# A recurrent-attention and lookup-table FFN block on one core: first gates turned by TensorE, statistics two slots ahead, sums of LN(x)^T at their own products, lookup steps dealt out anew

## The chip, the cores and the metric

The kernel runs on one core of a Trainium2 chip, in one launch. The metric is device time in microseconds (us). The kernel before was run three times: 2121.52, 2121.64 and 2123.93 us, median 2121.64.

## The reference, cut to what matters

```
x: (8, 1024, 512) fp32
xn  = (x - mean) / sqrt(var + 1e-5)                        # LN over the 512
# attention: D = 128, three decays
q, k_i, v_i = xn @ Wq, xn @ Wk[i], xn @ Wv[i];  gate = softmax(xn @ Wg)
w_i[t, s] = sigmoid(decay_logits[i]) ** max(s - t - 1, 0) * (s > t)
s   = sum_i gate[..., i] * ((q @ k_i^T) * w_i) @ v_i;  s = s @ Wo * out_scale
# FFN whose weights are table look-ups: w = lut[idx], lut of 16, idx (1376, 512) and (512, 1376)
g   = silu(down(silu(gate(xn)) * up(xn)))
out = x + s * g
```

Everything is fp32.

## The kernel before, in words

The kernel has two phases. Phase 1 (some 600 us) normalises and transposes x, makes the projections, runs the attention recurrence and builds the FFN weights from the table into DRAM. Phase 2 (the other 1500 us) is the FFN with the weights streamed back, and the output. Matrix products are by Strassen's scheme in Winograd's form: seven products of halves, with sums of the operands made beforehand. The diff touches phase 1 alone.

Phase 1 walks through batches b = 0 to 8 and, in each, through eight *slots* k = 0 to 7, one chunk of 128 tokens each, last chunk first (c = 7 - k). In a slot generators are advanced by hand, each by a step at a time:

- `newer`, `project(b)`, three steps per slot. Step 1: `transpose(c)` (four transposes `pt` on TensorE, ScalarE copies them to `xnT`), `normalize(c - 1)`, `statistics(c - 2)`, loads of x. Step 2, from slot 4 on: a product of `features(1)`. Step 3: `values(c)` (`pv`, copied to `v_sb` by ScalarE) and a further product of `features(1)`. In slot 4 also the softmax of the gates of tokens 512 to 1023.
- `ending`, the second half of `project(b - 1)`: in slots 0 to 3 the same for `features(0)`, whose products run while the next batch is transposed.
- `older`, `chunks(b - 1)`, three steps per slot: transposes `pk` of the keys, scaled by ScalarE into `ks` (L630); then `psc` (scores), VectorE's `pr` (L636), and for the next chunk `ga` (L611) by VectorE and `qb` (L615) by GpSimd; then the state product `pu` (needs `ks`) and the output `po` (needs `pr`), copied by ScalarE (L659, L663, L670).
- `weights`, the table look-ups: 396 steps in all. A look-up of one block is three bit masks (L218), one index step (L221), eight leaves (L225) and seven selects (L242), all on VectorE, most of them over 128 x 1024; after it come steps in which only GpSimd works (the Strassen sums, L272 to L301). `build_some(n)` takes n of these steps; it stands in three places of a slot.
- `following`, the start of `project(b + 1)`: first loads and statistics of the next batch.

`features(hf)` is one Strassen product of q and the three k for 512 tokens. Its products run in the order 1, 5, 6, 2, 7, 3, 4, one per step, thus two per slot over four slots; they accumulate in PSUM banks `pa`, `pe`, `pb`, `pa`, `pc`, `pe`, `pc`. Their right-hand operands are quarters of LN(x)^T or the sums `t1` (L494, for product 5), `t2` (L498, for 6), `t3` (L503, for 7) and `t4` (L509, for 4) that VectorE makes; VectorE also adds `c22` (L516, after product 7) and `c12` (L519, after product 3). `there` is a store of these for phase 2.

`statistics` of batches from 1 on are two passes of ScalarE (L411, L412) and two small steps of GpSimd that give `rstd` (L413, L414); `normalize` is two ScalarE steps (L421, L422).

The gates, softmaxed as 128 tokens x 12, are needed as 12 rows broadcast to all partitions: stored to DRAM element by element (L458), then read back by a broadcast (L462). `defer(n, ...)` issues something n `tick()`s later; a slot has three ticks.

The order on TensorE, VectorE, ScalarE and GpSimd is the order in which the program is traced (`keep_order` ties each instruction to the one before). SyncE's queue is tied so up to slot (0, 3) alone; after that the framework's planner places its DMAs.

Of the kernel before, what the change touches and what calls it, by code (L numbers as in the profile page):

```python
# [9 lines left out]
F32 = mybir.dt.float32  # L10
# [7 lines left out]
P = 128  # L18
# [30 lines left out]
def recurrent_block(ctx: ExitStack, tc, x, wq, wk, wv, wo, wg, decay_logits, out_scale, lut, gidx, uidx, didx, out):  # L49
# [84 lines left out]
    def defer(parts, issue):  # L134
        later.append([parts, issue])
# [241 lines left out]
    def project(b, pools, sides, kept):  # L377
# [61 lines left out]
        def softmax(hf):  # L439

            n = NC // NHALF
            logits = gt[:, ts(hf, n), :]
            g = small.tile([P, n, NI], F32, name=f"g{b}_{hf}", tag="g")
            red = small.tile([P, n, 1], F32, name=f"red{b}_{hf}", tag="red")
            nc.vector.tensor_reduce(red, logits, AX.X, ALU.max)
            nc.vector.tensor_tensor(g, logits, red.to_broadcast([P, n, NI]), ALU.subtract)
            nc.scalar.activation(g, g, AF.Exp)
            yield
            sm = small.tile([P, n, 1], F32, name=f"sm{b}_{hf}", tag="sm")
            nc.vector.tensor_reduce(sm, g, AX.X, ALU.add)  # L450
            nc.vector.reciprocal(sm, sm)
            nc.vector.tensor_tensor(g, g, sm.to_broadcast([P, n, NI]), ALU.mult)
            gates.append(att.tile([P, n * NI, P], F32, name=f"ga{b}_{hf}", tag="ga"))
            there = gT_d[b][ts(hf, n * NI), :]

            def write():
                with nc.allow_non_contiguous_dma(reason="1536 words"):
                    nc.sync.dma_start(out=there.rearrange("k p -> p k"), in_=g.rearrange("p c i -> p (c i)"))  # L458

            ga = gates[-1]  # L460
            defer(2, write)
            defer(6, lambda: nc.sync.dma_start(out=ga, in_=there.partition_broadcast(P)))  # L462

        def features(hf):

            qk[hf] = att.tile([P, NI + 1, U], F32, name=f"qk{b}_{hf}", tag=f"qk{hf}", bufs=1)  # L470
            c11, c12, c21, c22 = (qk[hf][:, 2 * j : 2 * j + 2, ts(c, H)] for j in (0, 1) for c in (0, 1))
            ts_ = tp.tile([P, 4, 2, H], F32, name=f"ts{b}_{hf}", tag=f"ts{hf}")
            b11, b12, b21, b22 = (xnT[:, 2 * v : 2 * v + 2, ts(2 * hf + c, H)] for v in (0, 1) for c in (0, 1))
            t1, t2, t3, t4 = (ts_[:, k] for k in range(4))
            a11, a12, s3, a22 = (wqk_sb[:, 2 * v : 2 * v + 2, ts(j, 2 * D)] for j in (0, 1) for v in (0, 1))
            s1, s2, s4 = (wqs[:, k] for k in range(3))
            lhs = {1: a11, 2: a12, 3: s4, 4: a22, 5: s1, 6: s2, 7: s3}
            rhs = {1: b11, 2: b21, 3: b22, 4: t4, 5: t1, 6: t2, 7: t3}
            pa, pb, pe, pc = (p_a.tile([P, 2, H], F32, name=f"{r}{b}_{hf}", tag=r) for r in ("pa", "pb", "pe", "pc"))

            def product(ps, k, start=False):
                for j in range(2):
                    for v in range(2):
                        nc.tensor.matmul(  # L484
                            ps[:, j, :],
                            lhsT=lhs[k][:, v, ts(j, D)],
                            rhs=rhs[k][:, v, :],
                            start=start and j == 0 and v == 0,
                            stop=False,
                            skip_group_check=True,  # L490
                        )

            there = xs_d[b][:, :, ts(hf, H)]
            nc.vector.tensor_tensor(t1, b12, b11, ALU.subtract)  # L494
            yield
            product(pa, 1, True)
            nc.scalar.copy(pb, pa)
            nc.vector.tensor_tensor(t2, b22, t1, ALU.subtract)  # L498
            nc.sync.dma_start(out=there[:, 0:4, :], in_=xnT[:, :, ts(2 * hf, H)])
            yield  # L500
            product(pe, 5, True)
            nc.scalar.copy(c21, pe)
            nc.vector.tensor_tensor(t3, b22, b12, ALU.subtract)  # L503
            nc.sync.dma_start(out=there[:, 4:6, :], in_=b22)
            yield
            product(pb, 6)
            nc.scalar.copy(pc, pb)
            nc.scalar.copy(c12, pb)
            nc.vector.tensor_tensor(t4, b21, t2, ALU.subtract)  # L509
            defer(2, lambda: nc.sync.dma_start(out=there[:, 6:14, :], in_=ts_.rearrange("p a b u -> p (a b) u")))  # L510
            yield
            product(pa, 2)
            nc.scalar.copy(c11, pa)
            yield
            product(pc, 7)
            nc.vector.tensor_tensor(c22, pc, c21, ALU.add)  # L516
            yield
            product(pe, 3)
            nc.vector.tensor_tensor(c12, pe, c12, ALU.add)  # L519
            yield  # L520
            product(pc, 4)
            nc.scalar.copy(c21, pc)
            yield
# [3 lines left out]
        def load_to(c):  # L527
            nonlocal ahead
            while ahead >= max(c, 0):
                load(ahead)  # L530
                ahead -= 1

        if b == 0:
            load_to(NC - 1)
            yield
            load_to(NC - 4)
        else:
            load_to(NC - 4)
        statistics(NC - 1)
        if b > 0:  # L540
            yield
            load_to(NC - 5)
        normalize(NC - 1)
        statistics(NC - 2)
        yield
        lag = 1 if b == 0 else 0
        for k in range(NC):
            c = NC - 1 - k
            transpose(c)
            if c > 0:  # L550
                normalize(c - 1)
            if c > 1:
                statistics(c - 2)
            if (b, k) != (0, 0):
                load_to(c - 5)
            if b == 0 and k == 0:
                warm_up(5)
            yield
            if k == NC // 2:
                if lag:  # L560
                    values(c + 1)
                    lag = 0
                of_half = features(1)
                next(of_half)
            if k >= NC // 2:
                next(of_half)
            half = softmax(1) if k == NC // 2 else iter(())
            next(half, None)
            yield
            next(half, None)  # L570
            if k >= lag:
                values(c + lag)
            if k >= NC // 2:
                next(of_half, None)
            yield
# [99 lines left out]
    def phase_1():  # L675
        nonlocal small, p_a, p_c, p_r
        with (
# [22 lines left out]
            def build_some(n):  # L700
                for _ in range(n):
                    next(weights, None)
# [12 lines left out]
            for b in range(B + 1):  # L715
                following = project(b + 1, pools, sides, kept) if b + 1 < B else iter(())
                older = chunks(b - 1, (chk, blp), kept) if b else iter(())
                for k in range(NC):

                    short = b > 0 and k % 4 == 3  # L720
                    busy = (b > 0 or k >= NC // 2) and b < B
                    swap = (b, k) == (1, 0)
                    tick()
                    next(newer, None)
                    next(older, None)
                    next(setup, None)
                    build_some((b, k) > (0, 0) and 1 + (0 < b < B) - short)
                    next(more, None)
                    tick()
                    if k < NC // 2:  # L730
                        for _ in range(2):
                            next(ending, None)
                    next(newer, None)
                    build_some(busy * (1 + (b > 0) - short))

                    next(newer if swap else older, None)
                    build_some(busy * (2 + (b > 0) + (b > 0 and k % 4 == 0)))
                    if k < NC // 2:
                        next(ending, None)
                    if k >= NC - 2:  # L740
                        next(following, None)
                    tick()
                    next(older if swap else newer, None)
                    next(older, None)
                    if (b, k) == (0, 3):
                        sums_of_weights(wqk_sb, wqs)
                        keep_order(tc, seen, (mybir.EngineType.SP,))
                for g in (older, ending):
                    for _ in g:
                        pass  # L750
                ending, newer = newer, following
# [669 lines left out]
```

## Time and profile before

| what | value |
|---|---|
| median of three runs | 2121.64 us |
| the profiled execution | 2122.92 us |
| its span, first to last instruction | 2121.0 us |
| instructions in the span | 32177 |
| mean granted TensorE clock | 0.996 |
| spacing of slots without a wait, from transpose to transpose | 9.50 us; 7.78 from slot 3 to 4; 6.78 after slot 7 |
| slot (1, 0) | 44.40 to 61.34, 16.95 us |

The times in the profile count from the span's start. PE is TensorE's matmul, PEld its weight load, DVE VectorE, ACT ScalarE, POOL GpSimd, SP SyncE. L434 is line 434 of the kernel. A line `A <- B: 12.8, 6, 5.1` in a list of waits says that A's engine stood idle 12.8 us before A, in 6 places, at most 5.1 us at once, until B was done. Lines of a timeline have start, duration, engine, line, operation and tiles, and in brackets the idle time before.

### The profile page before, as it was taken

The page shows a single profiled execution, that of the slowest core. Times are in us where ns is not written, and L with a number is a line of the kernel's source. Part 1 is how long each engine was busy: PE and PEld are TensorE (multiplying, and loading weights), DVE is VectorE, ACT ScalarE, POOL GpSimd, SP SyncE. Part 2 cuts the span into 40 slices and gives each one's busy share as a digit, 9 for nine tenths or more (in the row PEclk, how much of TensorE's full clock was granted, in tenths as well). Part 3 has the DMA queues.
Part 4 walks back from the last instruction along what each step waited for, and adds up shares of the span by engine and source line. Part 5 has one row for each costly group of instructions (what it writes and reads, how often), then busy time and mean ns, then how long its engine had stood idle before and what let it go on. Part 6 is the DMA issues. An engine that isn't in the chain of part 4 may idle for free.

```text
span 2121.0 us, 32177 instructions
## 1 busy us (share of the span) xinstructions
PE 2090.8 (99%) x11690; PEld 1756.3 (83%) x11690; DVE 1440.2 (68%) x2214; ACT 943.8 (44%) x2115; POOL 1038.9 (49%) x1050
## 2 busy tenths in 40 slices
PE   9999999999999999999999999999999999999999
PEld 6778777888878888888879888887978888797877
DVE  7789887799735775566567556655755675675557
ACT  4657765776534424423441442244145324423531
POOL 3555555364544537516542752655275256527432
PEclk9999999999999999999999999999999999999999
DMA  8575686647764654463455446344644634464443
GB/s 189 159 167 189 144 202 188 152 151 158 158 198 152 231 185 152 157 241 129 155 190 191 144 152 246 131 153 166 215 146 158 242 124 158 165 217 147 153 153 109
DMA packets 186163, 361.51 MB, mean 170 GB/s; under 512 B 52467, under 2 KB 123766, under 8 KB 186006
## 3 DMA queue, kind: packets, MB, share of 16 engines
q1 hardware_dynamic: 171446, 335.20, 51.1%
q0 software_dynamic: 4480, 14.68, 1.7%
q10 hardware_dynamic: 10080, 9.58, 1.5%
q8 instruction: 93, 1.52, 0.3%
q14 instruction: 64, 0.52, 0.1%
HBM read 282.87 MB, written 76.55 MB: 169 GB/s over the span
## 4 chain that ended last, share of the span: by engine, by line
PE 88%; DVE 5%; DMA 2%; POOL 2%; ACT 1%; issue 1%; SPq 0%; DVEq 0%; POOLq 0%; ACTq 0%
PE s L865 33%; PE sE L865 6%; PE pv L434 5%; PE s12d L1119 5%; PE s21d L1119 5%; PE s11d L1119 5%; PE fs L813 3%; PE pd L1232 3%; PE ps L1239 3%; PE po L658 2%; PE sEd L1119 2%; PE pc L484 2%; PE pe L484 2%; PE pa L484 2%; PE fsE L813 1%; DMA x<-in_x 1%
## 5 line engine op out<-in xcount | busy, mean ns | idle before, releaser
L865 PE MATMUL s<-xs,wq 128*128 128x256 f32 x3264 | 731.2, 379 | 0.0
L865 PEld LDWEIGHTS s<-xs,wq 128*128 128x128 f32 x3264 | 619.5, 190 | 95.9 <-issue 8.4
L888 DVE TENSOR_TENSOR s<-s,e 128x512 f32<-128x512 f32 x136 | 95.1, 699 | 204.3 <-ACT s L887 204.2
L1203 POOL TENSOR_TENSOR cu<-cu 128x256 f32<-128x256 f32 x32 | 34.8, 1087 | 306.7 <-DVE cl L1202 304.5
L434 PE MATMUL pv<-wvg_sb,xnT 128*128 128x387 f32 x512 | 177.4, 488 | 0.0
L796 POOL TENSOR_TENSOR xs<-xs 128x256 f32<-128x256 f32 x224 | 170.9, 790 | 7.1 <-PE fs L813 2.5
L892 DVE TENSOR_TENSOR sE<-s,e 128x512 f32<-128x512 f32 x136 | 95.0, 699 | 104.6 <-PE s L865 104.6
L956 POOL TENSOR_TENSOR u<-u,e 128x512 f32<-128x512 f32 x64 | 79.9, 1271 | 149.1 <-DVE u L952 130.6
L883 ACT COPY e<-sE 128x512 f32<-128x512 f32 x136 | 79.6, 585 | 139.4 <-PE sE L865 137.1
L865 PE MATMUL sE<-xs,wq 128*128 128x256 f32 x544 | 139.6, 379 | 0.0
L434 PEld LDWEIGHTS pv<-wvg_sb,xnT 128*128 128x128 f32 x512 | 94.2, 190 | 53.7
L960 POOL TENSOR_TENSOR h<-h,u 128x512 f32<-128x512 f32 x64 | 80.1, 1273 | 112.5 <-DVE u L967 104.8
L615 POOL TENSOR_TENSOR qb<-ga,q_tab 128x384 f32<-128x384 f32 x56 | 79.7, 1422 | 104.4 <-DVE ga L611 89.7
L876 ACT COPY s<-s 128x512 f32<-128x512 f32 x136 | 77.5, 570 | 109.0 <-PE s L865 105.3
L887 ACT COPY s<-s 128x512 f32<-128x512 f32 x136 | 77.5, 570 | 97.3 <-PE s L865 97.3
L1119 PE MATMUL s12d<-wdd,z 128*128 128x128 f32 x896 | 118.4, 275 | 0.6 <-ACT s12d L1141 0.6
L865 PEld LDWEIGHTS sE<-xs,wq 128*128 128x128 f32 x544 | 103.4, 190 | 14.1
L1119 PEld LDWEIGHTS s12d<-wdd,z 128*128 128x128 f32 x896 | 109.0, 192 | 0.8 <-ACT s12d L1141 0.8
L225 DVE TENSOR_SCALAR leaf<-idx,lut_x,lut_sb 128x1024 int32<-128x1024 int32 (+2 forms) x119 | 104.4, 900 | 0.0
L413 POOL TENSOR_SCALAR rstd<-rstd 128x1 f32<-128x1 f32 x56 | 24.6, 439 | 157.9 <-ACT junk L412 156.4
L242 DVE COPY_PREDICATED leaf<-bit,leaf 128x1024 f32<-128x1024 uint8 (+2 forms) x68 | 88.5, 1302 | 1.6
L1243 POOL TENSOR_TENSOR gx<-gx,cu 128x512 f32<-128x512 f32 x32 | 40.7, 1277 | 82.0 <-DVE cu L1241 64.5
(260 smaller groups left out, 4535.3 us busy)
## 6 DMA issues: line engine op xcount, KB each, us to landing
wq<-quadd SPq DMA_DIRECT2D x112, 896.0 KB, 4.5
wdd<-wdd SPq DMA_DIRECT2D x56, 896.0 KB, 4.9
xs<-xsd SPq DMA_DIRECT2D x56, 512.0 KB, 7.1
wq<-quadd SPq DMA_DIRECT2D x48, 448.0 KB, 4.1
x<-in_x SPq DMA_DIRECT2D x64, 256.0 KB, 6.5
xsd<-ts SPq DMA_DIRECT2D x16, 1024.0 KB, 14.7
gx<-in_x SPq DMA_DIRECT2D x64, 256.0 KB, 5.8
out<-gx POOLq DMA_DIRECT2D x56, 256.0 KB, 2.3
```

The source lines that it names most:

```text
L225: nc.vector.tensor_scalar(o.bitcast(I32), iv, lut_x[:rows, k, :], lut_i[:rows, k, 0:1], ALU.bitwise_and, ALU.bitwise_xor,)
L242: nc.vector.copy_predicated(o, bits[level - 1][:rows, :n], t[:rows, :n])
L434: nc.tensor.matmul(pv, lhsT=xnT[:, v, ts(c, P)], rhs=wvg_sb[:, v, :], start=(v == 0), stop=(v == NV - 1))
L484: nc.tensor.matmul(ps[:, j, :], lhsT=lhs[k][:, v, ts(j, D)], rhs=rhs[k][:, v, :], start=start and j == 0 and v == 0, stop=False, skip_grou ...
L796: nc.gpsimd.tensor_tensor(o, x1, x2, ALU.subtract)
L813: nc.tensor.matmul(ps, lhsT=w[:, 2 * W_OF[k] + n, :m], rhs=xs[:, X_OF[k], 2 * n : 2 * n + 2, :], start=start and n == 0, stop=stop and n == 1,
L865: nc.tensor.matmul(self.t[n][:, ts(a, H)], lhsT=self.w[:, a, (0, 1, 6, 3, 4, 5, 2)[i - 1], :], rhs=self.xs[:, X_OF[self.ks[a]], D_OF[i], : ...
L888: nc.vector.tensor_tensor(self.t[1], self.t[1], self.e, ALU.add)
L892: nc.vector.tensor_tensor(self.t[3], self.t[2], self.e, ALU.add)
L956: nc.gpsimd.tensor_tensor(o[:, n], o[:, n], other[:, n], ALU.add)
L960: nc.gpsimd.tensor_tensor(of_h(half, n), of_h(half, n), two(other[:, n]), ALU.mult)
L1119: nc.tensor.matmul(self.t[n][:, ts(a, P)], lhsT=self.lhs[i][:, e, ts(a, P)], rhs=self.w[:, e, D_OF[i], :], start=start and a == 0 and e == ...
```

## The change

Four things. The gates of batch 0's first half (the second 512 tokens) are transposed by TensorE, copied by ScalarE and stored as 12 rows; the others stay. Statistics of batches from 1 on are made two slots before their `normalize` instead of one; for that `following` starts at slot 5 instead of 6, and it now stands at the end of the slot. `t2`, `t3` and `t4` are each issued one step ahead of the product that reads them (at products 5, 2 and 3), `t4` behind `c12`. The look-up steps of batches 1 to 7 are dealt as (1, 1, 4), (1, 2, 5), (1, 2, 4), (1, 2, 3) to the three places of the slots k % 4 = 0 to 3; before they were (2, 2, 4), (2, 2, 3), (2, 2, 3), (1, 1, 3). The special order in slot (1, 0), where `values` came before the scores, is dropped.

```diff
+            def turn():
+                pg = p_c.tile([n * NI, P], F32, name=f"pg{b}_{hf}", tag="c")
+                nc.tensor.transpose(pg, g.rearrange("p c i -> p (c i)"), ident)
+                gs = small.tile([n * NI, P], F32, name=f"gs{b}_{hf}", tag="gs", bufs=1)
+                nc.scalar.copy(gs, pg)
+                nc.sync.dma_start(out=there, in_=gs)
...
-            defer(2, write)
+            if (b, hf) == (0, 1):
+                defer(3, turn)
+            else:
+                defer(2, write)
...
             product(pa, 1, True)
             nc.scalar.copy(pb, pa)
-            nc.vector.tensor_tensor(t2, b22, t1, ALU.subtract)
...
             product(pe, 5, True)
             nc.scalar.copy(c21, pe)
-            nc.vector.tensor_tensor(t3, b22, b12, ALU.subtract)
+            nc.vector.tensor_tensor(t2, b22, t1, ALU.subtract)
...
             product(pb, 6)
             nc.scalar.copy(pc, pb)
             nc.scalar.copy(c12, pb)
+            yield
+            product(pa, 2)
+            nc.scalar.copy(c11, pa)
+            nc.vector.tensor_tensor(t3, b22, b12, ALU.subtract)
+            yield
+            product(pc, 7)
+            nc.vector.tensor_tensor(c22, pc, c21, ALU.add)
+            yield
+            product(pe, 3)
+            nc.vector.tensor_tensor(c12, pe, c12, ALU.add)
             nc.vector.tensor_tensor(t4, b21, t2, ALU.subtract)
             defer(2, lambda: nc.sync.dma_start(out=there[:, 6:14, :], in_=ts_.rearrange("p a b u -> p (a b) u")))
-            yield
-            product(pa, 2)
...
             load_to(NC - 4)
-        statistics(NC - 1)
-        if b > 0:
+            statistics(NC - 1)
             yield
             load_to(NC - 5)
-        normalize(NC - 1)
-        statistics(NC - 2)
+            normalize(NC - 1)
+            statistics(NC - 2)
+            yield
+            statistics(NC - 3)
         yield
+        before = 2 if b == 0 else 3
...
-            if c > 1:
-                statistics(c - 2)
+            if c >= before:
+                statistics(c - before)
...
-                    short = b > 0 and k % 4 == 3
-                    busy = (b > 0 or k >= NC // 2) and b < B
-                    swap = (b, k) == (1, 0)
+                    if b == 0:
+                        steps = (k > 0, k >= NC // 2, 2 * (k >= NC // 2))
+                    elif b < B:
+                        steps = ((1, 1, 4), (1, 2, 5), (1, 2, 4), (1, 2, 3))[k % 4]
+                    else:
+                        steps = (1, 0, 0)
...
-                    build_some((b, k) > (0, 0) and 1 + (0 < b < B) - short)
+                    build_some(steps[0])
...
-                    build_some(busy * (1 + (b > 0) - short))
-                    next(newer if swap else older, None)
-                    build_some(busy * (2 + (b > 0) + (b > 0 and k % 4 == 0)))
+                    build_some(steps[1])
+                    next(older, None)
+                    build_some(steps[2])
                     if k < NC // 2:
                         next(ending, None)
-                    if k >= NC - 2:
+                    tick()
+                    next(newer, None)
+                    next(older, None)
+                    if k >= NC - 3:
                         next(following, None)
-                    tick()
-                    next(older if swap else newer, None)
-                    next(older, None)
```

More of the change, by code (lines that the diff above doesn't have):

```diff
@@ L508, in features @@
             nc.scalar.copy(c12, pb)
-            nc.vector.tensor_tensor(t4, b21, t2, ALU.subtract)
-            defer(2, lambda: nc.sync.dma_start(out=there[:, 6:14, :], in_=ts_.rearrange("p a b u -> p (a b) u")))
             yield
@@ L519, in features @@
             nc.vector.tensor_tensor(c12, pe, c12, ALU.add)
+            nc.vector.tensor_tensor(t4, b21, t2, ALU.subtract)
+            defer(2, lambda: nc.sync.dma_start(out=there[:, 6:14, :], in_=ts_.rearrange("p a b u -> p (a b) u")))
             yield
@@ L536, in project @@
             load_to(NC - 4)
+            statistics(NC - 1)
+            normalize(NC - 1)
+            statistics(NC - 2)
         else:
             load_to(NC - 4)
-        statistics(NC - 1)
-        if b > 0:
+            statistics(NC - 1)
             yield
             load_to(NC - 5)
-        normalize(NC - 1)
-        statistics(NC - 2)
+            normalize(NC - 1)
+            statistics(NC - 2)
+            yield
+            statistics(NC - 3)
         yield
+        before = 2 if b == 0 else 3
         lag = 1 if b == 0 else 0
```

## The prediction

> **What bounds the kernel now.** I read the page first, then busy time in stretches, then who TensorE waits for, then the timelines of single slots.
>
> The engine row of the page:
>
> ```profile
> PE 2090.8 (99%) x11690; PEld 1756.3 (83%) x11690; DVE 1440.2 (68%) x2214; ACT 943.8 (44%) x2115; POOL 1038.9 (49%) x1050
> ```
>
> TensorE is busy 99% of the span. The number of matmuls changes by one, so the change can move only what TensorE loses between matmuls. The busy times by stretch show where that is (columns: stretch, its length, busy us and instructions of PE, PEld, DVE, ACT, POOL, granted clock, DMA share, GB/s):
>
> ```profile
> 44.00:130.00 86.00, 75.70 (x411) 62.79 (x410) 68.27 (x86) 49.72 (x133) 42.14 (x39) 0.94 0.63 180
> 130.00:353.00 223.00, 215.03 (x1228) 178.27 (x1227) 200.03 (x245) 149.68 (x397) 123.63 (x111) 1.00 0.69 173
> 353.00:430.00 77.00, 73.57 (x417) 61.28 (x417) 56.67 (x88) 51.23 (x138) 27.90 (x31) 0.98 0.65 171
> 430.00:570.00 140.00, 139.94 (x803) 116.72 (x802) 127.20 (x156) 95.44 (x253) 78.02 (x67) 1.00 0.66 159
> ```
>
> TensorE lacks 10.3, 8.0, 3.4 and 0.1 us: 21.8 us, all in phase 1. The modelled end of a matmul hides some 0.16 us of each of 11 gaps (spacing of starts against the usual): 1.8 us. The granted clock is 0.5 for 6.8, 3.4 and 3.4 us after three of the gaps; without its part that lies in a gap that is 5.4 us of matmul time. So **29 us** can be won, no more. VectorE is busy 74 to 91% in these stretches, so the order in its queue decides.
>
> Waits of TensorE, and one of ScalarE, in the first 600 us (total, times, longest):
>
> ```profile
> PE po L658 <- DVE pr L636: 12.8, 6, 5.1
> PE pu L644 <- ACT ks L630: 5.6, 2, 2.9
> ACT shift L421 <- POOL rstd L414: 20.1, 7, 6.5
> ```
>
> `po` waits for `pr`, queued on VectorE behind lookup steps. `pu` waits for `ks`, queued on ScalarE behind `shift`, which waits for GpSimd's `rstd`.
>
> **What the change removes.**
> *Gates by TensorE.* SyncE issues the word-wise store of batch 0's first gates at 29.91 and can issue the broadcast only at 43.29; it lands at 49.01. VectorE idles 3.8 us for it, `t1` comes late, and `pe` waits 1.8 us. Turned, the store is 12 rows of 512 bytes. The trace has no such store; bounds are `out<-gx` (2.3 us) and `wdd` (4.9 us). With 5.7 us for the broadcast it lands at 38 to 42 (I take 40), before slot (1,0) at 44.4. Gain 1.8. Added are one transpose (0.11 us of spacing), queued before `pv`, a ScalarE copy (`bl`, of a like size: 0.27) and a wait of SyncE for it; TensorE pays 0.2 at most, since `g` is ready at 27.7 and the place is reached at 28.8.
> *No swap in slot (1,0).* `psc` and `pr` now stand ahead of four lookup steps: the 5.1 us wait at 59.90 goes, with 2.0 of clock.
> *Lookup steps spread.* Per four slots 8,7,7,5 become 6,8,7,6, and the slot with softmax, `t1`, `t2` is lightened by two: the five other `po` waits (7.7) and 1.7 of clock go.
> *Statistics two slots ahead.* `rstd` gets a slot (9.5 us) more, over the longest 6.5: the waits at `pu` and `pk` (5.6 and 1.5) and 1.6 of clock go. x tiles were issued over 25 us before their use from batch 2 on, so loads stay covered.
> Listed waits, clock, and the hidden 1.8 make the 29 us.
>
> **What it adds, first: p4 waits for t4.** `t4` moves from product 6 to behind `c12`, which needs product 3; product 4 needs `t4` and follows after only `pu`, `po`, `pt` (and `pk`). VectorE in such a half before (start, duration), and TensorE's product 4 under it:
>
> ```profile
> 486.98 0.69 DVE L516 TENSOR_TENSOR qk<-pc,qk 128x512 f32<-128x512 f32 x1 [1.14 <-ACT shift L421]
> 487.58 0.80 DVE L225 TENSOR_SCALAR leaf<-idx,lut_x,lut_sb 128x1024 int32<-128x1024 int32 x1
> 488.42 1.31 DVE L242 COPY_PREDICATED leaf<-bit,leaf 128x1024 f32<-128x1024 uint8 x1
> 489.63 0.54 DVE L636 TENSOR_TENSOR pr<-psc,w_tab 128x384 f32<-128x384 f32 x1
> 490.09 0.55 DVE L611 TENSOR_TENSOR ga<-ga,qk 128x384 f32<-128x384 f32 x1
> 490.55 1.30 DVE L242 COPY_PREDICATED wgu<-bit,leaf 128x1024 f32<-128x1024 uint8 x1
> 491.74 2.21 DVE L225 TENSOR_SCALAR leaf<-idx,lut_x,lut_sb 128x1024 int32<-128x1024 int32 x2
> 493.87 0.68 DVE L519 TENSOR_TENSOR qk<-pe,qk 128x512 f32<-128x512 f32 x1
> ```
>
> ```profile
> 494.16 1.89 PE L484 MATMUL pc<-ts,wqk_sb 128*128 128x256 f32 x8
> ```
>
> VectorE had idled 1.14 us, so `c22` (L516) starts as early as product 7 lets it. `c12` (L519) ends at 494.55, 0.4 after product 4 has begun: today no harm. After the change four steps, not three, stand between `ga` and `c12` (one more: 0.84 for a leaf to 1.21 for a select, I take 0.95), and `t4` (0.65) follows: it ends at 496.2, and product 4 waits 2.0 us. Nothing hides this: TensorE is in order. I laid the 396 steps into the slots of the new table, 14 halves under load. Two fall on steps of GpSimd alone and one on the shorter last block: 0.3 us together. For the other 11, from `c22` to `c12`: the steps' spacing (leaf 0.73, select 1.18, bit 0.62) + 1.54 for `c22`, `pr`, `ga` + 0.95 for GpSimd's interference, the excess that ten halves of before show. With 1.6 for `c12`, `t4` and signals this is 8.7 to 10.3 us from the end of product 7; TensorE arrives after 7.45 (no `pk`) or 7.77. Waits of 1.1 to 2.5, mean 1.85: **20.7 us** with the three.
>
> The interference in a row:
>
> ```profile
> 231.70 1.44 POOL L615 TENSOR_TENSOR qb<-ga,q_tab 128x384 f32<-128x384 f32 x1 [3.01 <-DVE ga L611]
> ```
>
> It took 1.00 us alone (at 226.46); here it ran beside two leaves that lasted 2.21 together instead of 1.5. Both gave way by halves.
> [...]
>
> **Second: t2 and t3 come one product before their use.** `t3`: 0.27 + `pr` and `ga` 0.94 + five steps 4.0 to 4.8 + 0.95 + 0.68 after `psc` makes 6.8 to 7.6, TensorE arrives after 7.1; `t2` 6 to 8.2 against 7.8. Waits of 0 to 0.5 in 28 places; I take 4 us, bounds 1 and 12 (if lateness adds up).
>
> **Third: ScalarE's statistics of the next batch move to the slot's end**, behind `po` and ahead of `xnT`, for which `pv` waits. The end of such a slot before:
>
> ```profile
> 413.47 0.27 ACT L659 COPY bl<-po 128x128 f32<-128x128 f32 x1 [1.42 <-PE po L658]
> 413.63 0.48 ACT L663 COPY R<-pu 128x384 f32<-128x384 f32 x1
> 414.15 1.09 ACT L670 ACTIVATE pu<-pu,c_tab 128x128 f32<-128x128 f32 x3
> 415.17 0.59 ACT L428 COPY xnT<-pt 128x512 f32<-128x512 f32 x1
> ```
>
> `xnT` ends at 415.76 and `pv` starts at 416.44: 0.68 spare. One statistics takes 1.58 (417.44 to 419.02): slot 6 loses 0.9 in six batches, **5.4 us**. In slot 7 a normalisation comes too (2.6 against 1.5 spare), but product 4 waits longer there. Bounds 2 and 9.
>
> **Fourth:** batch 0 has no older chunks between its products, so `t4` (41.2) makes product 4 (40.05) wait 1.1, and ScalarE may wait for the first x tile: 2 us, bounds 1 and 4. VectorE's waits for a `wgu` buffer (three, 10.1 us, longest 4.1) stay; I keep 2 us of `po` and `t4` for them.
>
> **Sum.** The profiled execution took 2122.9 (span 2121.0), 1.3 over the median of 2121.6. 2122.9 - 29 + 20.7 + 4 + 5.4 + 2 + 2 = 2128. A measurement of this kernel can tell about 0.2% (4.2 us) from no change.
>
> **Rivals.**
> *A, the forecast:* 2128, own range 2120 to 2135. 0.5.
> *B, faster:* VectorE is lighter before `t4`. Interference falls with fewer GpSimd steps beside it, as where `c22` to `c12` took 3.9 and 5.0 us. Then 0.95 drops out: 11 x 0.9 = 10 for `t4`, 1 for `t2`, `t3`, 5 for ScalarE, 2 for batch 0: 2122.9 - 29 + 18 = 2112. For it: 430 to 570 us lost nothing at 91% VectorE. Against: that stretch shows the 7 us intervals too. It decides from where `t4` waits under 1.2 us on average. 0.22.
> *C, VectorE's lateness adds up:* `t2`, `t3` cost 12, and four waits come near 2.7 us and halve the clock, at 1.7 each: 2122.9 - 29 + 20.7 + 12 + 5.4 + 4 + 7 = 2143, I put it at 2140. 0.2.
> For the clock the rows are: idle of 2.73 us at 364.48 was followed by half clock, 2.86 at 287.12 was not.
> [...]
> *D, the change doesn't do what it says:* SyncE's order still delays the gates, or GpSimd's sums hold `rstd` beyond two slots (at 275.28 to 283.36 one stood 8.1 us): 6 us come back: 2134. 0.08.
>
> **Numbers.** Slower: 0.36 of A, C, 0.07 of D: 0.63. Same: 0.14 of A, 0.02 of B, 0.01 of D: 0.17. Faster: 0.20 of B. The range runs from B's middle to C's: 2111 to 2141.
>
> **What would show it.** Right: `pc` waits for `ts` about 1.9 us in some 11 places and is TensorE's costliest wait; `po` on `pr` and `pu` on `ks` nearly gone; slot (1,0) near 9.5 us instead of 16.95; `pv` waits for `xnT` once per batch; no wait at 49 for `ga`. Wrong: `pc` waits under 10 us in total, or `po` still waiting for `pr`.

## The result: slower by 1.0%, beyond the range

The changed kernel takes 2143.89 us (median of five runs, 2141.78 to 2147.56), the kernel before 2121.64 beside it (2121.52 to 2124.08). The ratio is 1.0102, 95% interval 1.0087 to 1.0117. The side was forecast, the size was not: 2128 was said, with a range up to 2141. The time is rival C's, and so is most of the mechanism.

The profiled execution took 2147.56 us (span 2145.4), 3.7 over the median. Its runs scatter more than those of the kernel before, and the granted clock goes with them: 0.995 in this run, 0.998 in the fastest (2141.78), 0.996 in the other three.

The engine row of the page:

```profile
PE 2101.0 (98%) x11691; PEld 1759.2 (82%) x11691; DVE 1432.8 (67%) x2214; ACT 944.4 (44%) x2116; POOL 1028.5 (48%) x1050
```

One matmul more, as expected. Busy time by stretch, cut at about the same places of the work as in the prediction (start to slot (1,0); batch 1; batches 2 to 4; 5; 6 to within slot (7,7)):

```profile
0.00:51.00 51.00, 44.67 (x186) 32.52 (x187) 36.37 (x76) 16.69 (x35) 18.57 (x28) 0.97 0.84 198
51.00:131.30 80.30, 74.61 (x411) 60.96 (x411) 70.25 (x85) 50.34 (x132) 39.89 (x39) 0.98 0.57 161
131.30:370.00 238.70, 222.36 (x1230) 182.30 (x1229) 196.55 (x246) 149.73 (x396) 125.08 (x113) 0.98 0.62 165
370.00:443.00 73.00, 71.74 (x412) 59.49 (x410) 58.56 (x89) 49.76 (x132) 23.09 (x28) 1.00 0.54 167
443.00:588.00 145.00, 136.94 (x786) 113.59 (x783) 113.43 (x150) 95.05 (x252) 70.98 (x66) 1.00 0.51 144
```

Slot (1,0) begins 7 us later (51.46 after 44.40), batch 1 has become shorter (80.3 us after 86), batches 2 to 4 longer (238.7 after 223), and the last batches, where nothing had been lost, now lose 8 us. The granted clock is below 1 in three of the five stretches. TensorE's waits in phase 1:

```profile
PE pc L495 <- DVE ts L529: 17.8, 11, 3.4
PE pv L434 <- ACT xnT L428: 7.9, 10, 3.2
PE pb L495 <- DVE ts L513: 5.1, 4, 2.8
PE pc L495 <- DVE ts L522: 3.5, 4, 2.7
PE po L674 <- DVE pr L652: 1.4, 1, 1.4
```

Of the old waits in the prediction's list only the last line is left, and every new one is among those forecast: `t4` (L529), `xnT`, `t2` (L513), `t3` (L522).

To account for all of it I compare the spacing of matmul starts with their usual spacing (0.112 us for 128 columns, 0.216 for 256, 0.326 for 387, 0.429 for 512), over the first 700 us. An excess of up to the usual spacing in a half-clock stretch is put down to the clock, the rest of an excess over 0.18 us to the wait that ended it, small ones to "scatter". (So a wait is some 0.16 larger here than in the list above.)

| lost by TensorE, us | before | after |
|---|---|---|
| po on pr, qb; pu on ks; pk; pe on t1; first product of phase 2; start | 25.1 | 3.1 |
| products on t4 | 0 | 19.9 (12 places) |
| products on t2 and t3 | 0 | 10.1 (9) |
| pv on xnT | 0 | 9.5 (10) |
| half clock | 5.3 (3 stretches) | 9.0 (6) |
| scatter | 3.2 | 6.3 |
| sum | 33.5 | 57.9 |

The difference, 24.4 us, is that of the spans.

The half from which the wait for `t4` was worked out looks like this now (VectorE, then TensorE):

```profile
501.93 0.69 DVE L525 TENSOR_TENSOR qk<-pc,qk 128x512 f32<-128x512 f32 x1 [2.31 <-PE pc L495]
502.54 1.30 DVE L242 COPY_PREDICATED wgu<-bit,leaf 128x1024 f32<-128x1024 uint8 x1
503.72 0.81 DVE L225 TENSOR_SCALAR leaf<-idx,lut_x,lut_sb 128x1024 int32<-128x1024 int32 x1
504.44 0.55 DVE L652 TENSOR_TENSOR pr<-psc,w_tab 128x384 f32<-128x384 f32 x1
504.91 0.55 DVE L627 TENSOR_TENSOR ga<-ga,qk 128x384 f32<-128x384 f32 x1
505.37 0.81 DVE L225 TENSOR_SCALAR leaf<-idx,lut_x,lut_sb 128x1024 int32<-128x1024 int32 x1
506.22 1.99 DVE L242 COPY_PREDICATED leaf<-bit,leaf 128x1024 f32<-128x1024 uint8 x1
508.25 1.32 DVE L242 COPY_PREDICATED wgu<-bit,leaf 128x1024 f32<-128x1024 uint8 x1
509.44 0.82 DVE L225 TENSOR_SCALAR leaf<-idx,lut_x,lut_sb 128x1024 int32<-128x1024 int32 x1
510.16 0.70 DVE L528 TENSOR_TENSOR qk<-pe,qk 128x512 f32<-128x512 f32 x1
510.76 0.70 DVE L529 TENSOR_TENSOR ts<-xnT,ts 128x512 f32<-128x512 f32 x1
```

```profile
511.52 0.70 PE L495 MATMUL pc<-ts,wqk_sb 128*128 128x256 f32 x2 [1.33 <-DVE ts L529]
```

Six lookup steps stand between `c22` and `c12`, VectorE never pauses, and `t4` ends at 511.46. VectorE had waited 2.31 us *ahead* of `c22`: there is time in the slot, but in the wrong place. From `c22`'s start to the end of `t4` it is 9.5 us; the forecast had 9.2 for this half, and a wait of 2.0 where 1.33 is shown (1.49 by spacing).

### The profile page after: what moved, and what is told of

It is laid out like the page before. It is cut to its first block, busy times and chain, and to the rows that moved or that the text cites. A ratio compares the mean times of both kernels' runs of the same rounds, so it can differ in the third digit from the quotient of the medians.

```text
span 2145.4 us, 32141 instructions
## 1 busy us (share of the span) xinstructions
PE 2101.0 (98%) x11691; PEld 1759.2 (82%) x11691; DVE 1432.8 (67%) x2214; ACT 944.4 (44%) x2116; POOL 1028.5 (48%) x1050
## 4 chain that ended last, share of the span: by engine, by line
PE 88%; DVE 7%; ACT 2%; POOL 2%; issue 1%; DMA 0%; DVEq 0%; POOLq 0%; ACTq 0%
PE s L884 33%; PE sE L884 5%; PE pv L434 5%; PE s12d L1138 5%; PE s21d L1138 5%; PE s11d L1138 5%; PE fs L832 3%; PE po L674 3%; PE pd L1251 3%; PE ps L1258 3%; PE sEd L1138 2%; PE pc L495 2%; PE pa L495 2%; DVE leaf L225 2%; PE pe L495 1%; PE psc L650 1%
## 5 line engine op out<-in xcount | busy, mean ns | idle before, releaser
L225 DVE TENSOR_SCALAR leaf<-idx,lut_x,lut_sb 128x1024 int32<-128x1024 int32 (+2 forms) x119 | 98.9, 849 | 0.0
L242 DVE COPY_PREDICATED leaf<-bit,leaf 128x1024 f32<-128x1024 uint8 (+2 forms) x68 | 93.6, 1377 | 1.4
L495 PE MATMUL pc<-ts,wqk_sb 128*128 128x256 f32 x256 | 67.6, 411 | 21.5 <-DVE ts L529 17.8
```

What stands on the lines that cost most here:

```text
L225: nc.vector.tensor_scalar(o.bitcast(I32), iv, lut_x[:rows, k, :], lut_i[:rows, k, 0:1], ALU.bitwise_and, ALU.bitwise_xor,)
L242: nc.vector.copy_predicated(o, bits[level - 1][:rows, :n], t[:rows, :n])
L495: nc.tensor.matmul(ps[:, j, :], lhsT=lhs[k][:, v, ts(j, D)], rhs=rhs[k][:, v, :], start=start and j == 0 and v == 0, stop=False, skip_grou ...
```

## The experiments

"Before" in this section is 2124.1 to 2124.9 us, the kernel before run beside each set.

### Sums back in their old places: `u_sums`

The changed kernel, with `t2`, `t3`, `t4` at products 1, 5, 6:

```diff
             product(pa, 1, True)
             nc.scalar.copy(pb, pa)
+            nc.vector.tensor_tensor(t2, b22, t1, ALU.subtract)
...
             nc.scalar.copy(c21, pe)
-            nc.vector.tensor_tensor(t2, b22, t1, ALU.subtract)
+            nc.vector.tensor_tensor(t3, b22, b12, ALU.subtract)
...
             nc.scalar.copy(c12, pb)
+            nc.vector.tensor_tensor(t4, b21, t2, ALU.subtract)
...
-            nc.vector.tensor_tensor(t3, b22, b12, ALU.subtract)
...
-            nc.vector.tensor_tensor(t4, b21, t2, ALU.subtract)
```

The store of the sums moves with `t4`.

> The changed kernel with t2, t3 and t4 back where they were (at products 1, 5 and 6); lookup table, statistics, gates as changed. Theory: pc and pb wait for no sum; 19.6 (t4) + 9.9 (t2, t3) + 9 (clock) us go: 2104 to 2110, below the kernel before. What remains is pv on xnT (9.5) and 2 or so on po. Rival (the lookup table of the change was cut for the late sums, with early sums VectorE is late at pr): po on pr comes back with 10 us or more, 2118 or above.

Measured: 2117.47, 0.9975 of before (0.9964 to 0.9985). Undoing this one part takes 28 us off, and what is left of the change is a small gain. No stretch of phase 1 runs at half clock (mean granted clock 0.999 in the profiled run). TensorE's waits:

```profile
PE pv L434 <- ACT xnT L428: 11.6, 13, 2.2
PE po L674 <- DVE pr L652: 5.0, 4, 1.8
```

The late sums are the loss; but the time is 7 to 13 us above what the theory said (2.5 of it because the kernel before, too, took 2124.1 here and not 2121.6), and the rival has half a point: with the sums early `po` waits for `pr` again (5 us, not 10). And `pv` waits longer for `xnT` than in the changed kernel (13.7 against 9.5 by spacing), with waits in slots 6 and 7 of all six batches; the waits on `t4` in slot 7 no longer cover it.

### Only t4 one step earlier: `u_t4`

```diff
             nc.vector.tensor_tensor(c22, pc, c21, ALU.add)
+            nc.vector.tensor_tensor(t4, b21, t2, ALU.subtract)
...
             nc.vector.tensor_tensor(c12, pe, c12, ALU.add)
-            nc.vector.tensor_tensor(t4, b21, t2, ALU.subtract)
```

The store of the sums moves with it.

> The changed kernel with one edit: t4 is made one step earlier, behind c22 at product 7, instead of behind c12 at product 3. t2 and t3 stay one product ahead. Theory (the new waits of products on their sums, and the half clock that follows the long ones, are the loss): the wait of pc on t4 (17.8 us, 11 places) goes, with most of the six half-clock stretches: about 25 us less, 2116 to 2122; t2 and t3 still cost some 9. Rival (VectorE as a whole is the limit and the place of the sums does not matter): the wait only moves, to product 7, psc/po or the next sum, and the time stays above 2135.

Measured: 2140.20, ratio 1.0077 (1.0062 to 1.0093): some 5 us better than the changed kernel, not 25, and on the rival's side of 2135. The wait for `t4` is gone from the list, the others have grown:

```profile
PE pv L434 <- ACT xnT L428: 11.1, 12, 3.3
PE pb L495 <- DVE ts L513: 10.3, 6, 5.4
PE pc L495 <- DVE ts L522: 4.5, 5, 3.2
PE fs L832 <- issue: 4.2, 1, 4.2
PE po L674 <- DVE pr L652: 3.2, 3, 1.7
```

The theory fell short here. A wait of TensorE let VectorE catch up; with `t4`'s 17.8 us away VectorE was later at the next things that TensorE needs: the wait for `t2` went from 5.1 to 10.3 us, that for `xnT` from 7.9 to 11.1. The dearest case, `t2` 5.4 us late at 103.82, shows how lateness builds up on VectorE:

```profile
92.58 3.98 DVE L218 TENSOR_SCALAR bit<-idx 128x1024 uint8<-128x1024 uint8 x2
96.59 2.46 DVE L221 TENSOR_SCALAR idx<-idx 128x1024 int32<-128x1024 int32 x1
101.04 0.81 DVE L225 TENSOR_SCALAR wgu<-idx,lut_x,lut_sb 128x1024 int32<-128x1024 int32 x1 [1.99 <-POOL pair L300]
101.77 0.16 DVE L450 TENSOR_REDUCE sm<-g 128x4 f32<-128x12 f32 x1
101.96 0.18 DVE L451 RECIPROCAL sm<-sm 128x4 f32<-128x4 f32 x1
102.17 0.17 DVE L452 TENSOR_TENSOR g<-g,sm 128x12 f32<-128x12 f32 x1
102.26 1.50 DVE L513 TENSOR_TENSOR ts<-xnT,ts 128x512 f32<-128x512 f32 x1
```

Beside GpSimd's sums the two bit steps take 2.57 and 1.49 us instead of 0.68 each; then the first leaf of a block waits 2 us for the buffer that GpSimd's `pair` sum still reads; the softmax and `t2` stand behind it. The half clock is no less either (10.7 us by spacing). But 4.2 us of waiting and 3.3 of the clock belong to phase 2's first product `fs`, which the changed kernel did not lose; that is a matter of SyncE, which `best_a` takes up, and not of VectorE.

### The start of the next batch: `u_follow` and `u_sums_follow`

```diff
                     if k < NC // 2:
                         next(ending, None)
+                    if k >= NC - 3:
+                        next(following, None)
                     tick()
                     next(newer, None)
                     next(older, None)
-                    if k >= NC - 3:
-                        next(following, None)
```

On the changed kernel:

> The changed kernel with the start of the next batch (statistics, normalisation by ScalarE) ahead of the slot's last third, as before, instead of at its end; it still starts at slot 5. Theory: pv's waits for xnT in slots 6 and 7 of batches 1 to 6 go (6 us); the wait of 3.2 us in slot (0,6) stays, since the first x tile of batch 1 lands no earlier: 2136 to 2140. Rival (product 4's wait for t4 takes the time back, as that is later in the same slots): less than 2 us gained.

Measured: 2148.72, 1.0115 (1.0100 to 1.0130): no gain. `pv` waits for `xnT` once instead of ten times, as the theory has it (7.9 us to 3.3), and `t4`'s wait takes it back (17.8 to 22.1 us). This is the rival.

With the sums in their old places too:

> Both: sums back at products 1, 5, 6 and the next batch's start ahead of the slot's last third. Theory: the gains add, 2098 to 2104. Rival of the lookup table: 2115 or above, with po on pr.

Measured: 2116.49, 0.9962 (0.9948 to 0.9976). Only 1 us better than `u_sums`, the rival's side: the waits of `pv` in slots 6 and 7 are gone, but the one in slot (0,6) has grown to 4.8 us and `po` on `pr` from 5.0 to 7.8.

### Lookup steps behind the sums: `a_last`

This one separates two readings of "the sums come late": that they are issued one product ahead, or that lookup steps stand in front of them. The sums stay where the change put them.

```diff
                     next(older, None)
-                    build_some(steps[2])
                     if k < NC // 2:
                         next(ending, None)
                     tick()
                     next(newer, None)
+                    build_some(steps[2])
                     next(older, None)
```

> The changed kernel with one edit: the third group of lookup steps (3 to 5 per slot) is queued behind the slot's second product and its sum, not ahead of them. The sums stay at products 5, 2 and 3. Theory (the sums are late because three to five lookup steps stand ahead of them in VectorE's queue, not because they are issued one product ahead): pc and pb on ts fall from 30 us to under 6, the half clock goes; VectorE now waits some 2 us per slot for product 3 or 5 and is later at pr, so po on pr rises to 5 to 12: 2112 to 2125. Rival (the sums are late because their place is one product ahead, whatever stands before them): 2138 or above.

Measured: 2126.39, 1.0007 (0.9997 to 1.0017): 1.4 us above the theory's range and far from the rival's 2138. The products' 30 us of waiting for `t2`, `t3`, `t4` are down to 1.2, and the clock is whole (1.000 in the profiled run). `po` on `pr` rises to 7.5 by spacing, `pv` on `xnT` to 12, and `pe` now waits 4.0 for `t1`: the time is that of the kernel before, lost at other places. The same kind of half:

```profile
485.55 0.56 DVE L627 TENSOR_TENSOR ga<-ga,qk 128x384 f32<-128x384 f32 x1
488.49 0.69 DVE L528 TENSOR_TENSOR qk<-pe,qk 128x512 f32<-128x512 f32 x1 [2.38 <-PE pe L495]
489.10 0.68 DVE L529 TENSOR_TENSOR ts<-xnT,ts 128x512 f32<-128x512 f32 x1
```

VectorE now idles 2.38 us for product 3, and `t4` follows at once. Here one product's lead is enough, as nothing else stands in the queue.

### Each part alone on the kernel before

`o_sums` moves the three sums as the change does; `o_steps` takes the new lookup table and drops the special order in slot (1,0); `o_stats` makes the statistics two slots ahead, but starts the next batch ahead of the slot's last third; `o_turn` turns the first gates. Their edits are those parts of the change's diff.

> The kernel before with only the sums moved (t2, t3, t4 at products 5, 2, 3). Theory (the late sums by themselves are the loss): some 25 to 30 us more than before, 2146 to 2155; pb and pc wait for ts 25 us or more, and the waits of po on pr shrink, since VectorE gets the time of the new waits. Rival (only together with the new lookup table, which puts six steps between c22 and t4, are the sums late): less than 10 us more, under 2134.

> The kernel before with only the new lookup table, and without the special order in slot (1,0). Theory (prediction's terms: po's waits on pr 12.8 and clock 3.7 go; the gates still land at 49, so psc in slot (1,0) waits some 2.5 us): 2106 to 2112. Rival (with t3 and t4 early, slots 4 and 5 are still overfull): po still waits 5 us or more, 2115 or above.

> The kernel before with only the statistics two slots ahead, the next batch's start at slot 5 but ahead of the slot's last third as before. Theory: pu's and pk's waits (7.1) and 1.6 of clock go, slot (0,6) pays 3 to 5 for the first x tile: 2116 to 2121. Rival (GpSimd's sums hold rstd back two slots as well): pu on ks stays, no gain.

> The kernel before with only the first gates turned by TensorE. Theory: the broadcast lands by 41 instead of 49; pe's wait on t1 (2.2 us) goes, po's wait in slot (1,0) stays or shrinks, since VectorE no longer idles 3.8 us: 2 to 6 us less, 2118 to 2122. Rival (SyncE's queue delays the store and broadcast all the same): no gain.

| kernel | us | ratio to before (95%) |
|---|---|---|
| o_sums | 2147.96 | 1.0115 (1.0100 to 1.0130) |
| o_steps | 2127.85 | 1.0017 (1.0008 to 1.0027) |
| o_stats | 2121.89 | 0.9996 (0.9987 to 1.0006) |
| o_turn | 2119.80 | 0.9986 (0.9969 to 1.0002) |

With the sums alone moved, the products wait 26.9 us for them and `po` only 4.4 for `pr`; the new table is not needed for that, and the time is that of the theory. But not all of it is theirs: 10.9 us of `o_sums` are a single wait of `psc`, because ScalarE stood 13.76 us at `bl` for a DMA, and the longest stretch of half clock (13.65 us, from 380.37) begins in that wait. Why the DMA was late was not followed up, so what the sums cost in time on the kernel before stays open.

The three other parts do not bring what the prediction booked for them. `o_steps` shows it best:

```profile
PE po L658 <- DVE pr L636: 7.9, 7, 1.5
PE pu L644 <- ACT ks L630: 4.2, 1, 4.2
PE psc L634 <- DVE ga L611: 4.1, 2, 3.2
```

The 5.1 us wait of slot (1,0) is gone, but the five others (7.7 us) have become seven of 7.9; `psc` now waits for the late gates, and the clock is halved in three stretches, as before. That is this run's rival. In `o_stats` `pu`, `pk` no longer wait, but `po` waits 14.0 and `psc` 3.1 for `bl`. `o_turn` lost `pe`'s wait, and its runs scatter (2114.67 to 2129.21), so that no gain is established.

### Versions that might beat both: `best_a`, `best_b`, `best_c`

`best_a` is the changed kernel with `t2`, `t3`, `t4` at products 1, 5, 2, `following` as in `u_follow`, and batch 1's first statistics at slot 6:

```diff
             load_to(NC - 4)
-            statistics(NC - 1)
+            if b > 1:
+                statistics(NC - 1)
             yield
             load_to(NC - 5)
-            normalize(NC - 1)
-            statistics(NC - 2)
+            if b == 1:
+                statistics(NC - 1)
+            else:
+                normalize(NC - 1)
+                statistics(NC - 2)
             yield
+            if b == 1:
+                normalize(NC - 1)
+                statistics(NC - 2)
             statistics(NC - 3)
```

> The changed kernel with t2, t3, t4 at products 1, 5, 2, the next batch's start ahead of the slot's last third, and for batch 1 alone the first statistics back at slot 6. Theory: against u_sums_follow the wait of 4.8 us on x in slot (0,6) and its half clock go (6.6), and po's waits on pr fall from 7.8 to about 4 since t4 is behind slot 5's pr: 2104 to 2109. Rival (VectorE's total is the limit): 2112 or above.

Measured: 2118.27, 0.9972 (0.9963 to 0.9982), on the rival's side of 2112. Slot (0,6) is mended, but `po` waits 9.1 us for `pr` where 4 were expected, and phase 2's first product `fs` waits 4.8 us and runs at half clock after it. SyncE's own waits between 560 and 640 us point to the cause:

```profile
SPq L473 <- DMA gTd<-g: 9.9, 1, 9.9
SPq L812 <- DMA xsd<-ts: 7.8, 1, 7.8
```

SyncE stands 9.9 us on the word-wise store of the last gates, the last store of sums goes out behind it, and phase 2's loads of x wait for that.

`best_b` therefore turns the last gates too (`best_c` turns all, with `if True`):

```diff
-            if (b, hf) == (0, 1):
+            if (b, hf) in ((0, 1), (B - 1, 0)):
                 defer(3, turn)
```

> best_a, and the gates of the last batch's second half (tokens 0 to 511) turned by TensorE too. Theory: SyncE no longer stands 10 us on that word-wise store ahead of the last store of sums, for which phase 2's loads of x wait; the 5 us wait at phase 2's first product and its 2.8 of clock go: 2109 to 2113. Rival (phase 2's first weights are late by themselves): no gain, 2116 or above.

> best_a with all sixteen gates turned by TensorE: 16 transposes (0.11 us each) and copies more, no word-wise store, SyncE freed of some 150 us of waiting. Theory: as best_b, and 0 to 3 us more from earlier loads, less 1.8 for the transposes: 2108 to 2114. Rival (ScalarE's copies and the PSUM places delay pv and psc): 2116 or above.

`best_b`: 2111.26, 0.9936 (0.9921 to 0.9951), faster than both kernels, as the theory said. `fs` is down to 0.5 us, which confirms SyncE's part. `best_c`: 2135.78, 1.0052 (1.0037 to 1.0067), the rival:

```profile
PE pv L434 <- DVE pr L659: 16.9, 8, 4.3
```

`pg` takes one of the three PSUM places that `pt`, `pk`, `psc`, `pv` and `po` share. In the slots of all eight waits a `pg` stands ahead of `pv`; `pv` then waits until VectorE's `pr`, late in its queue, has read `psc`, and so takes the place of `psc`. `pg` itself waits 7.4 us as well. In slot (0,5) and in batch 8, where `best_b` has its two, no such wait follows.

## Why the prediction missed, point by point

The step that failed is the second half of the sum, what the change adds. It was put at 34 us and came to 52. Half clock behind the new waits stood there at nothing and took 9.0 us; `t2` and `t3` stood at 4 us and took 10.1. The other three terms (`t4`, `xnT`, batch 0) were right together: 28.1 forecast, 29.4 measured. Scatter rose by 3. Which waits would come, and where, was in the main forecast rightly. The removal of 29 us held, but it was booked to the wrong parts.

**What bounds the kernel: right.** TensorE's work did not change, phase 2 did not either, and everything went through the matmuls' gaps in phase 1.

**The 29 us that go: right in the changed kernel, wrong as a price of those parts.** Old waits fell from 25.1 to 3.1. But the prediction booked them to the gates, the dropped swap, the lookup table and the statistics. Where those parts stand without the late sums (`u_sums`) they win 7 us net. In the changed kernel the new waits of TensorE gave VectorE the time to be punctual at `pr`: where they are taken away (`u_sums`, `a_last`), `po` waits again (5.0 and 6.3 us, where the changed kernel had 1.4). What does not hold is "the five other `po` waits (7.7) and 1.7 of clock go", as a gain of the table: in `o_steps` the 5.1 us wait went with the swap, and 7.9 us were left beside it.

**t4: right in mechanism and sum.** 20.7 forecast in 14 halves and 1.1 in batch 0; 18.7 and 1.2 measured. The lookup steps between `c22` and `t4` carried it, and `a_last` shows that it is those steps. One by one the waits were not right: 1.1 to 2.5 us were forecast in 11 halves, and 0.3 to 3.6 came. That they averaged out is partly luck, and half clock followed three of the long ones.

**t2 and t3: mis-sized.** 4 us taken, 10.1 measured, near the upper bound of 12. Each half was summed as if VectorE entered it on time. It did not: at 181.75 product 6 waited 2.8 us for `t2`. Between `t1` (173.32) and `t2` (181.01) VectorE had the softmax, `pr`, `ga` and five lookup steps, one of them 1.98 us long beside `qb`, and no pause.

```profile
181.75 1.67 PE L495 MATMUL pb<-ts,wqs 128*128 128x256 f32 x6 [2.80 <-DVE ts L513]
```

**Half clock: left out of the forecast, the largest miss.** Rival C alone had it, for four waits near 2.7 us (7 us). Six waits were followed by half clock (three for `t4`, one each for `t2`, `t3` and `xnT`), 9.0 us in all, the shortest of them this:

```profile
588.30 2.87 PE L495 MATMUL pc<-ts,wqk_sb 128*128 128x256 f32 x8 [2.22 <-DVE ts L529]
```

Eight matmuls took 2.87 us instead of 1.89. A wait of 2.57 at 549.85 was not followed by it, as 2.86 at 287.12 before was not. So the length of a wait alone does not tell it. The traces show what goes with it. Within a trace the stretches of half clock start at multiples of 3.413 us from each other, to within 0.002 us: 39.72, 84.10, 183.08, 244.52, 312.79 and 589.27 here, 57.13, 111.74 and 364.33 in the trace of before. Cut the time into these windows, and look at TensorE's busy time (first after the length) and the clock (third from the end) around the two waits of 2.57 and 2.22 us:

```profile
544.90:548.31 3.41, 2.38 (x22) 2.15 (x20) 3.34 (x3) 1.79 (x7) 0.00 (x0) 1.00 0.00 0
548.31:551.72 3.41, 1.87 (x9) 1.67 (x10) 1.48 (x3) 3.34 (x10) 0.22 (x2) 1.00 0.30 108
551.72:555.13 3.41, 3.41 (x17) 2.32 (x16) 2.16 (x3) 0.86 (x3) 3.33 (x4) 1.00 1.00 353
585.86:589.27 3.41, 1.19 (x8) 0.87 (x6) 3.38 (x6) 0.96 (x3) 0.00 (x0) 1.00 0.45 158
589.27:592.68 3.41, 3.41 (x12) 2.95 (x11) 2.53 (x3) 0.59 (x1) 0.00 (x0) 0.50 0.85 303
```

The longer wait is split between two windows, 1.0 and 1.5 us idle, and nothing follows; the shorter one lies in one window, 2.2 us idle, and the next window has half the clock. The 2.86 us before are split into 1.6 and 1.3; the 2.73 at 364.48 put 2.6 into one window. In the first 700 us of these two traces, nine windows at full clock held more than 2.0 us idle (2.08 to 3.17), and each was followed by half clock; no other at full clock held more than 1.56, and none of those was. So a wait of more than 2 us was followed by half clock or not by where it fell; why, no run shows. Some of the waits with a mean of 1.85 and a spread should thus have been priced with it.

**xnT: 5.4 forecast in slot 6 of six batches, and part of the 2 us of batch 0; 9.5 measured.** Slot 6 took 4.0 (0.8 in four of the six batches), slot 7, not wholly covered by product 4's wait, 2.2 in three. The other 3.3 are slot (0,6), dearer than its bounds: there ScalarE stood for the first x tile.

```profile
37.20 0.63 ACT L411 ACTIVATE junk<-x 128x512 bf16<-128x512 f32 x1 [2.63 <-DMA x<-in_x]
```

```profile
39.29 4.56 PE L434 MATMUL pv<-wvg_sb,xnT 128*128 128x387 f32 x8 [3.18 <-ACT xnT L428]
```

The loads were traced a slot earlier and yet issued at 29.60, after 28.38 before, since SyncE stood 9.4 us at the decay table (7.9 before); only the statistics came earlier. With 3.3 us here, half clock behind it, and 1.2 for `t4`, "Fourth: 2 us" should have been 5 or more.

**The rivals.** B (interference falls away) did not come: the half shown took 9.5 us, and `t4`'s waits are 1.34 us over the 14 halves, above B's 1.2. C is nearly what happened: `t2` and `t3` took 10.1 of its 12, and half clock followed six waits and not four. D is out: `pu` waits nowhere for `ks`, and nobody waited for the broadcast, though it landed at 43.99, past the 38 to 42 of the prediction. (Its store went out only at 34.20, behind the loads of x.)

**A reading that was wrong.** "Both gave way by halves", of `qb` beside two leaves, does not hold. The first leaf, under `qb` from 231.70, took 0.81 us, as leaves without `qb` do (0.80 at 228.53). The second began at 232.20 under `qb` and ended 0.55 us after it (`qb` ended at 233.14), 1.49 us in all; `qb` in turn ended 0.86 us after the first leaf and took 1.44 (1.00 at 226.46, where it began under none). The last section has more rows of this. The 0.95 us that the sum took for it came from measured halves and is not touched.

Together: -29 held (the table has 25.1 and 5.3 before); the added terms, forecast at 34, came to 19.9 + 10.1 + 9.5 + 3.1 (old waits that stayed) + 9.0 = 52, and scatter rose by 3.

## What to carry to other kernels

An operand that an engine makes in the order of the program must not be placed by its consumer alone: count what stands ahead of it in its engine's queue, and put work that nobody waits for behind it, not before it (in `a_last` 30 us of waits for the sums became 1.2). When TensorE's waits are summed, the sum has to be carried from slot to slot, because here a wait removed made the helper engine later at the next place (`u_t4`: 17.8 us for `t4` went, 5.1 for `t2` became 10.3) and a wait added made it earlier (`po` on `pr`: 12.8 us before, 4.4 in `o_sums`); parts then have no prices of their own, and only parts tried alone show it. And waits of two microseconds should be priced with the half clock that may follow: here six stretches, 9.0 us, 1.5 each.

## What the runs showed that was not expected

- In the changed kernel half clock came after waits of 2.2 to 3.4 us, for 3.41 us each time, but not after 2.57. The windows of 3.41 us ahead of the six stretches held 2.08 to 3.17 us of idle time, the two around the wait of 2.57 held 1.03 and 1.54.
- A VectorE bit step took 2.57 us instead of 0.68 beside a GpSimd sum of 128 x 896. It ended 0.56 us after the sum did (at 94.59). In the changed kernel 39 of the 41 bit, index and leaf steps of 128 x 1024 that began under a GpSimd sum or `qb` in phase 1 ended 0.54 to 0.56 us after it, the other two, begun in its last 0.05 us, 0.63 us after it. `qb` was longer likewise: begun under a select at 176.08, it took 1.93 us instead of 1.00 and ended 0.84 us after it. Two rows of `u_t4`:

```profile
92.32 2.27 POOL L292 TENSOR_TENSOR pair<-pair,wgu 128x896 f32<-128x896 f32 x1
92.58 2.57 DVE L218 TENSOR_SCALAR bit<-idx 128x1024 uint8<-128x1024 uint8 x1
```

- Turned by TensorE, a store of 12 rows kept SyncE 5.0 us, against 12 for the word-wise one: still more than the 2.3 to 4.9 taken from other stores.
- One more small tile among the three PSUM places made `pv` wait 16.9 us (`best_c`), always for the reader of another tile that was late.
